# Cross-attention of layer 0 in a decoder kernel: another order of the first group's pieces, and the next stage's rows normalised apart from their turning

## The chip, the cores and the metric

The kernel runs on one core of a Trainium2 chip. The metric is the device time of one execution in microseconds. The time before the change is the median of three runs, 3578.55 us (3572.76 to 3597.9). One more execution was recorded by the hardware profiler; every view of the profile below is of that one.

The engines are named as the profile names them: PE multiplies matrices, and PEld is its loading of weights; DVE and ACT work element by element, ACT also by function tables; POOL is a third such engine; SP issues most of the DMAs. [...]

## The reference

A decoder of four layers on 16 sequences of 128 tokens with 256 features. Each layer has self-attention, cross-attention to a context of 128 x 192 per sequence, and a feed-forward part, each on the normalised x and added to x:

```python
x = x + _L0_attn_ref(_layernorm(x, axis=-1), ...)
x = x + _L0_xattn_ref(_layernorm(x, axis=-1), ctx_768, ctx_768, ...)
x = x + _L0_ffn_ref(_layernorm(x, axis=-1), ...)
...
```

The change lies in the second and at the start of the third of these. The cross-attention of layer 0 has 16 heads of 16 features. Queries come from x, keys and values from the context, each with weights and a bias. Queries and keys are divided by their lengths, over all 256 features, before the scores are taken; the softmax of the scaled scores weighs the values, and an output projection follows. The unnormalised query projection is added to that, and the sum is normalised over its features with a gain and a shift before it goes to x. The feed-forward part of layer 0 is a mixture of 32 experts and a shared one, with a router that picks eight experts for each token.

## The kernel before, in words

Tokens lie on the 128 partitions. The 2048 tokens form four groups of four sequences (`NG` = 4, `GB` = 4), so a group has 512 tokens (`GT`). x stays in on-chip memory, one tile for each group. Two kinds of PSUM buffers are used in this stage: `b1` makes single banks, four in turn, and `b2` makes double banks, two in turn.

The function `l0_xattn` gives `staggered` a prologue for each group, the scores, the exponentials and the combination of a sequence. The prologue of a group makes these pieces, in this order:

- the group's rows of x normalised (`h`, L546, on DVE);
- for two halves of the features: keys from the context (`kT`, PE), their bias (L555, DVE), their squares (`ksq`, L556, ACT);
- `h` turned by PE (`tr`), copied to `hT` by DVE (L112) and ACT (L114) in turn;
- the squared lengths of the keys, by matmuls with a single column of ones (`ksum`), clipped on DVE (L570);
- query projections of the four sequences (`qp`), their bias on DVE (L579), the sum of their squares on ACT (L580);
- lengths: maximum on DVE (L583), square root on ACT (L584), reciprocal on DVE (L585); queries divided by their lengths on ACT (`unit`, L588); output bias and shift added on POOL (L589, L590);
- values of two sequences (`v`), bias on DVE (L270);
- `unit` turned by PE (`utr`) and written as masked queries `qm`, one copy on DVE (L606), one on ACT (L607);
- values of the other two sequences.

The prologue is a generator. For group 0, `staggered` runs it to its end before anything else. For groups 1 to 3, it takes two pieces at each of the four steps of the group before. A step n takes the scores of sequence n (`st`), the last part of the combination of sequence n-3 (`proj`), the second of n-2 (`o16t`, with a reciprocal and a product `c` on DVE), a piece, the exponentials of sequence n on ACT (`e`), the first part of the combination of n-1 (`o`, copied to `oT` on ACT), another piece, and the third part of n-2 (`ctr`, copied to `cT` on DVE). After that come works that the dictionary `beside` names for this step. The last sequence of a group ends with four DVE instructions that update x (L631).

Matmuls of this stage go through `pinned` and `pinned_transpose`, which keep them in the order of the program text on PE. For the other engines a scheduler of the language orders the instructions by their dependencies and their place in the text, so an instruction can stand earlier than its line suggests.

The stage after it, `l0_ffn`, needs for each group the normalised rows of x, turned. `l0_ffn_rows(g)` does both: statistics on DVE (L653, L654), square root on ACT (L193), `nmean` on DVE (L656), rows `h` on ACT (L659), turning on PE (`tr`), copies to `hT` on ACT (L667). For groups 0 and 1 `staggered` calls it after steps 13 and 14; for groups 2 and 3 `l0_ffn` calls it after the router of groups 0 and 1. `l0_ffn` starts with the shared expert (e = -1): for each group `gate` and `up`, then `gs` on ACT (L758) and DVE (L759), then `down` of the group before, then the `router`.

The tile `h` has two buffers, which `h` of the prologue, `unit` and `h` of `l0_ffn_rows` take in turn; `hT` has five.

Of the kernel before, what the change touches and what calls it, by code (L numbers as in the profile page):

```python
# [9 lines left out]
F = mybir.dt.float32  # L10
BF = mybir.dt.bfloat16
# [6 lines left out]
P = 128  # L18
# [12 lines left out]
class Decoder:  # L31
    def __init__(self, ctx, tc, a, out):
        self.tc, self.nc, self.a, self.out = tc, tc.nc, a, out
        nc = self.nc
        pool = lambda name, bufs, **k: ctx.enter_context(tc.tile_pool(name=name, bufs=bufs, **k))
        self.const = pool("const", 1)
        self.wp = pool("weights", 1)
        self.hp = pool("hidden", 1)
        self.sm = pool("small", 4)
        self.open_psum()  # L40
        self.flip = 0
        self.l0_hT = []

        const = self.const

        self.x = []
        xv = a["x"].rearrange("(g b s) d -> g s b d", b=GB, s=P)
        for g in range(NG):
            xt = const.tile([P, GB, DM], F, tag=f"x{g}", name=f"x{g}")
            nc.sync.dma_start(out=xt, in_=xv[g])  # L50
            self.x.append(xt)
        self.col = const.tile([P, a["cols"].shape[1]], F, tag="cols", name="cols")
        nc.sync.dma_start(out=self.col, in_=a["cols"])

# [456 lines left out]
    def l0_xattn(self):  # L511
# [24 lines left out]
        with self.tc.tile_pool(name="l0x", bufs=1) as wk:  # L536
            bq, bv, bo = (self.brow(wk, f"L0_xattn_{n}") for n in ("bq", "bv", "bo"))

            def prologue(g):
# [9 lines left out]

                kT = wk.tile([P, 2, GT], F, tag="kT", name="kT", bufs=2)  # L550
                sq = self.hp.tile([P, 2, GT], F, tag="hT", name="ksq", bufs=5)
                for half in range(2):
                    ps = self.b1("kT")
                    products(ps, self.ctx_l(wk_, half * P, (half + 1) * P, slice(g * GT, (g + 1) * GT)))
                    nc.vector.tensor_scalar(kT[:, half, :], ps, self.c("L0_xattn_bk")[:, half : half + 1], None, ALU.add)  # L555
                    nc.scalar.activation(sq[:, half, :], kT[:, half, :], AF.Square)  # L556
                    yield
                hT = self.hp.tile([P, 2, GT], F, tag="hT", name="hT", bufs=5)
                for k in range(2):
                    ps = self.b1("tr")  # L560
                    for t in range(GB):
                        self.pinned_transpose(ps[:, T4(t)], h[:, t, k * P : (k + 1) * P])
                    self.evac(hT[:, k, :], ps)

                n = self.small([P, 2, GB], "lengths")
                ps = self.b1("ksum")[:, 0:GB]
                for t in range(GB):
                    products(ps[:, t : t + 1], [(sq[:, half, T4(t)], self.ones[:, 0:1]) for half in range(2)])

                nc.vector.tensor_scalar(n[:, 0], ps, 1e-24, 16.0, ALU.max, ALU.mult)  # L570
                yield
                if g % 2 == 0:
                    qps.append(self.slot([P, 2, GB, DM], "qp"))
                qp = qps[-1][:, g % 2]
                junk = wk.tile([P, DM], BF, tag="junk", name="junk", bufs=1)
                for t in range(GB):
                    ps = self.b1("qp")[:, 0:DM]
                    products(ps, [(hT[:, k, T4(t)], wq[:, k, :]) for k in range(2)])
                    nc.vector.tensor_tensor(qp[:, t, :], ps, bq, ALU.add)  # L579
                    nc.scalar.activation(junk, qp[:, t, :], AF.Square, accum_out=n[:, 1, t : t + 1])  # L580
                    if t == 1:
                        yield
                nc.vector.tensor_scalar(n[:, 1], n[:, 1], 1e-24, None, ALU.max)  # L583
                nc.scalar.activation(n, n, AF.Sqrt)  # L584
                nc.vector.reciprocal(n, n)  # L585
                u = self.hp.tile([P, GB, DM], F, tag="h", name="unit", bufs=2)
                for t in range(GB):
                    nc.scalar.activation(u[:, t, :], qp[:, t, :], AF.Copy, scale=n[:, 1, t : t + 1])  # L588
                nc.gpsimd.tensor_tensor(qp, qp, bo.unsqueeze(1).to_broadcast([P, GB, DM]), ALU.add)  # L589
                nc.gpsimd.tensor_tensor(self.x[g], self.x[g], beta.unsqueeze(1).to_broadcast([P, GB, DM]), ALU.add)  # L590
                yield
                v = []

                def values(t):
                    pairs = self.ctx_r(wv, 0, DM, slice(g * GT + t * P, g * GT + (t + 1) * P))
                    v.append(self.values32(wk, pairs, bv, products))

                values(0)
                values(1)
                yield  # L600
                qm = wk.tile([P, 2, 2, GT], F, tag="qm", name="qm", bufs=2)
                for half in range(2):
                    ps = self.b1("utr")
                    for t in range(GB):
                        self.pinned_transpose(ps[:, T4(t)], u[:, t, half * P : (half + 1) * P])
                    nc.vector.tensor_scalar(qm[:, half, 0, :], ps, self.par[:, 0:1], None, ALU.mult)  # L606
                    nc.scalar.activation(qm[:, half, 1, :], ps, AF.Copy, scale=self.par[:, 1:2])  # L607
                yield
                values(2)
                values(3)  # L610
# [2 lines left out]
            def combine(s, g, t, es):  # L613
# [25 lines left out]
                lambda s, t: self.scores16(s[0], s[1], T4(t), False),  # L639
                lambda s, t, st, nm: self.exponentials16(wk, st, s[2][:, t : t + 1], None),  # L640
                combine,
                {13: [lambda: self.l0_ffn_rows(0)], 14: [lambda: self.l0_ffn_rows(1)]},
            )

    def l0_ffn_rows(self, g):
# [12 lines left out]
        for t in range(GB):  # L658
            nc.scalar.activation(  # L659
                h[:, t, :], self.x[g][:, t, :], AF.Identity, scale=rs[:, t : t + 1], bias=nm[:, t : t + 1]  # L660
            )
        hT = self.hp.tile([P, 2, GT], F, tag="hT", name="hT", bufs=5)
        for k in range(2):
            ps = self.b1("tr")
            for t in range(GB):
                self.pinned_transpose(ps[:, t * P : (t + 1) * P], h[:, t, k * P : (k + 1) * P])
            nc.scalar.copy(hT[:, k, :], ps)  # L667
        self.l0_hT.append(hT)

    def l0_ffn(self):  # L670
# [20 lines left out]
        with self.tc.tile_pool(name="l0f", bufs=1) as wk:  # L691
# [82 lines left out]


            last, bias = None, None
            for e in range(-1, E):
                for g in range(NG):
                    now = first(e, g)
                    if last:  # L780
                        second(*last)
                    last = now
                    if e < 0:
                        router(g)
                        if g + 2 < NG:
                            self.l0_ffn_rows(g + 2)
                    if bias:
                        next(bias)
                        bias = None
                    if e == 1:  # L790
                        bias = biases(g)
                        next(bias)
# [1795 lines left out]
```

## Time and profile before

| what | value |
|---|---|
| time, median of three runs | 3578.55 us (3572.76 to 3597.9) |
| profiled execution: its time, its span | 3590.36 us, 3588.6 us |
| PE busy, share of the span | 3314.7 us, 92% |
| DVE, ACT, POOL busy | 59%, 40%, 12% |
| mean clock of PE in the span | 0.960 |
| first scores of this cross-attention start | 203.35 us |
| first `gate` of the feed-forward part starts | 340.03 us |

The span is from the first to the last instruction that the profiler saw; the execution's own time is 1.8 us longer. Times inside the span are counted from its start. In a timeline, a row is a run of like instructions on one engine: start, time from the start of the first to the end of the last, instruction, and in brackets how long the engine had been idle and which instruction ended that. A clock of 0.50 means that PE was granted half of its full clock in that stretch. Matmuls overlap, so rows of PE can begin before the row above has ended.

### The profile page before, as it was taken

The page shows a single profiled execution, that of the slowest core. Times are in us where ns is not written, and L with a number is a line of the kernel's source. Part 1 is how long each engine was busy: PE and PEld are TensorE (multiplying, and loading weights), DVE is VectorE, ACT ScalarE, POOL GpSimd, SP SyncE. Part 2 cuts the span into 40 slices and gives each one's busy share as a digit, 9 for nine tenths or more (in the row PEclk, how much of TensorE's full clock was granted, in tenths as well). Part 3 has the DMA queues.
Part 4 walks back from the last instruction along what each step waited for, and adds up shares of the span by engine and source line. Part 5 has one row for each costly group of instructions (what it writes and reads, how often), then busy time and mean ns, then how long its engine had stood idle before and what let it go on. Part 6 is the DMA issues. An engine that isn't in the chain of part 4 may idle for free.

```text
span 3588.6 us, 51453 instructions
## 1 busy us (share of the span) xinstructions
PE 3314.7 (92%) x20947; PEld 1791.9 (50%) x20947; DVE 2108.9 (59%) x4185; ACT 1428.4 (40%) x1925; POOL 424.4 (12%) x605
## 2 busy tenths in 40 slices
PE   7898999999998899998999998388999999999999
PEld 4665655555566566665555565252222222225656
DVE  5545444444554544468777544326999989964430
ACT  2356211111124422238555322024677767783221
POOL 5410000000003311110000110104000000002100
PEclk9989999999999999999999999597999999999989
DMA  2000000000010100010100000464202020000000
GB/s 78 1 23 14 14 22 18 18 23 18 28 49 2 38 1 1 1 42 8 46 1 13 3 1 1 169 209 130 35 16 32 12 31 11 11 1 26 1 8 18
DMA packets 90500, 105.46 MB, mean 29 GB/s; under 512 B 11380, under 2 KB 72694, under 8 KB 90006
## 3 DMA queue, kind: packets, MB, share of 16 engines
q1 hardware_dynamic: 79672, 89.71, 9.7%
q0 software_dynamic: 4224, 6.43, 0.6%
q10 hardware_dynamic: 6368, 6.03, 0.5%
q8 instruction: 165, 2.70, 0.3%
q14 instruction: 71, 0.58, 0.1%
HBM read 85.53 MB, written 16.60 MB: 28 GB/s over the span
## 4 chain that ended last, share of the span: by engine, by line
PE 79%; DVE 10%; ACT 5%; issue 3%; DMA 2%; POOL 1%; SPq 0%; POOLq 0%; ACTq 0%; DVEq 0%
PE acc L2120 7%; PE down L257 6%; PE gate L257 6%; PE up L257 6%; PE proj L257 6%; PE st L2120 5%; PE one L2120 4%; PE qT L168 4%; PE st L257 4%; PE o L257 2%; PE h L257 2%; DVE mx L2266 2%; PE rb L257 2%; PE v L1030 2%; PE fc L168 2%
## 5 line engine op out<-in xcount | busy, mean ns | idle before, releaser
L2266 DVE TENSOR_REDUCE mx<-one 128x1 f32<-128x512 f32 x1024 | 658.4, 686 | 58.9 <-PE one L2120 50.0
L2403 ACT ACTIVATE e<-st 128x1024 f32<-128x1024 f32 x512 | 497.1, 1021 | 209.4 <-PE st L2120 207.9
L758 ACT ACTIVATE gs<-gate,cols 128x512 f32<-128x512 f32 x132 | 90.7, 687 | 552.6 <-PE gate L257 552.5
L2120 PE MATMUL acc<-e,v 128*32 128x512 f32 x2048 | 285.6, 612 | 0.9 <-ACT e L2403 0.9
L2120 PE MATMUL st<-qp,kp 113*128 113x512 bf16 x1024 | 272.3, 386 | 5.9 <-DMA qp<-shifts 3.6
L772 DVE SCALAR_TENSOR_TENSOR x<-down,w_all,x 128x256 f32<-128x256 f32 x512 | 212.4, 478 | 110.6 <-PE down L257 110.4
L257 PE MATMUL down<-expert,gs 128*128 128x256 f32 x1056 | 250.1, 380 | 2.2 <-DVE gs L759 2.2
L257 PE MATMUL gate<-hT,expert 128*128 128x512 f32 x528 | 250.0, 596 | 0.0
L257 PE MATMUL up<-hT,expert 128*128 128x512 f32 x528 | 248.1, 592 | 0.0
L257 PEld LDWEIGHTS down<-expert,gs 128*128 128x128 f32 x1056 | 200.9, 190 | 85.8 <-issue 61.2
L759 DVE SCALAR_TENSOR_TENSOR gs<-up,cols,gs 128x512 f32<-128x512 f32 x132 | 99.0, 750 | 233.2 <-PE up L257 229.2
L2120 PE MATMUL one<-kp,qp 16*128 16x512 bf16 x1024 | 211.3, 396 | 3.7 <-DVE mx L2266 2.4
L2120 PEld LDWEIGHTS <-qp 16*128 16x128 bf16 x1024 | 48.8, 91 | 327.4 <-issue 322.6
L257 PEld LDWEIGHTS up<-hT,expert 128*128 128x128 f32 x528 | 100.3, 190 | 126.3 <-issue 126.3
L2120 PEld LDWEIGHTS <-kp 113*128 113x128 bf16 x1024 | 79.0, 98 | 143.9 <-issue 82.2
L1130 ACT COPY rb<-rb 128x512 f32<-128x512 f32 x64 | 37.5, 585 | 257.1 <-PE rb L257 257.1
L257 PEld LDWEIGHTS gate<-hT,expert 128*128 128x128 f32 x528 | 100.6, 192 | 70.8 <-issue 64.3
L1132 DVE TENSOR_TENSOR cT<-o,rb 128x512 f32<-128x512 f32 x64 | 44.3, 692 | 154.7 <-ACT rb L1130 154.7
L168 PE MATMUL qT<-hT,L_xattn_Wq 128*128 128x512 f32 x256 | 114.1, 598 | 6.9 <-DVE hT L112 4.5
L257 PE MATMUL o<-e,v 128*32 128x128 f32 (+1 forms) x2048 | 105.5, 279 | 12.6 <-DVE nm L294 11.8
L1439 DVE SCALAR_TENSOR_TENSOR xs<-xBC,cols,xs 128x508 f32<-128x508 f32 x144 | 106.0, 742 | 12.3 <-ACT xs L1435 9.0
L257 PEld LDWEIGHTS o<-e,v 128*32 128x32 f32 (+1 forms) x2048 | 81.5, 124 | 28.5 <-POOL e L335 12.3
(536 smaller groups left out, 5413.2 us busy)
## 6 DMA issues: line engine op xcount, KB each, us to landing
W<-in_L_ffn_W_dram SPq DMA_DIRECT2D x46, 512.0 KB, 5.2
expert<-in_L_ffn_Wg_dram SPq DMA_DIRECT2D x32, 128.0 KB, 2.1
expert<-in_L_ffn_Wu_dram SPq DMA_DIRECT2D x32, 128.0 KB, 2.5
expert<-in_L_ffn_Wd_dram SPq DMA_DIRECT2D x32, 128.0 KB, 2.5
parts<-parts SPq DMA_DIRECT2D x16, 256.0 KB, 2.5
qp<-parts SPq DMA_DIRECT2D x28, 128.0 KB, 3.8
kp<-parts SPq DMA_DIRECT2D x12, 256.0 KB, 8.6
hs<-zero SPq DMA_DIRECT2D x23, 128.0 KB, 1.9
```

What stands on the lines that cost most here:

```text
L168: self.nc.tensor.matmul(out, lhsT, rhs, start=i == 0, stop=i == n - 1 and bias is None)
L257: self.tc.keep_in_program_order(self.nc.tensor.matmul(*a, **k))
L758: nc.scalar.activation(gs, pg, AF.Silu, bias=bg)
L759: nc.vector.scalar_tensor_tensor(gs, pu, bu, gs, ALU.add, ALU.mult)
L772: nc.vector.scalar_tensor_tensor(xt, pd[:, t, :], w_all[:, o : o + 1], xt, ALU.mult, ALU.add)
L1030: nc.tensor.matmul(ps, l, r, start=True, stop=False)
L1130: nc.scalar.copy(rb, ps)
L1132: nc.vector.tensor_tensor(cT, po, rb, ALU.mult)
L1439: stt = lambda *a: pin(nc.vector.scalar_tensor_tensor(*a))
L2120: self.tc.keep_in_program_order(nc.tensor.matmul(*a, **k))
L2266: nc.vector.tensor_reduce(mx[:, t, kc, i : i + 1], pair[i], AX.X, ALU.max)
L2403: nc.scalar.activation(e[:, 2 * p : 2 * p + 2, :], ps, AF.Exp, scale=1.0 / 16.0)
```

## The change

The prologue's pieces become functions of their own: `keys(half)`, `turned()`, `key_lengths()`, `queries(t)`, `units()`, `values(t)`, `masked(u)`. For groups 1 to 3 they are called in the order of before, with the same places at which the generator yields. For group 0 they are called in another order: rows turned and queries first, then keys and their lengths, units, all four values, and masked queries last.

`l0_ffn_rows` is cut in two. It ends with the rows `h`, which it keeps in a dictionary; the new `l0_ffn_turn` turns and copies them. Groups 0 and 1 have their rows made after steps 10 and 12 and turned after steps 13 and 15; the rows of group 2 are made after step 16, those of group 3 at the start of the expert loop; these two are turned where both were done before. Tiles are the same as before, in shape and in number of buffers.

```diff
-        self.l0_hT = []
+        self.l0_h, self.l0_hT = {}, []
...
+                def keys(half):
                     ps = self.b1("kT")
                     products(ps, self.ctx_l(wk_, half * P, (half + 1) * P, slice(g * GT, (g + 1) * GT)))
                     nc.vector.tensor_scalar(kT[:, half, :], ps, self.c("L0_xattn_bk")[:, half : half + 1], None, ALU.add)
                     nc.scalar.activation(sq[:, half, :], kT[:, half, :], AF.Square)
-                    yield
...
+                def masked(u):
+                    for half in range(2):
+                        ps = self.b1("utr")
+                        for t in range(GB):
+                            self.pinned_transpose(ps[:, T4(t)], u[:, t, half * P : (half + 1) * P])
+                        nc.vector.tensor_scalar(qm[:, half, 0, :], ps, self.par[:, 0:1], None, ALU.mult)
+                        nc.scalar.activation(qm[:, half, 1, :], ps, AF.Copy, scale=self.par[:, 1:2])
+
+                if g == 0:
+                    turned()
+                    for t in range(GB):
+                        queries(t)
+                    keys(0)
+                    keys(1)
+                    key_lengths()
+                    u = units()
+                    for t in range(GB):
+                        values(t)
+                    masked(u)
+                    return qm, kT, n[:, 0], v, qp
+                keys(0)
+                yield
+                keys(1)
+                yield
+                turned()
+                key_lengths()
+                yield
+                queries(0)
+                queries(1)
+                yield
+                queries(2)
+                queries(3)
+                u = units()
+                yield
                 values(0)
                 values(1)
                 yield
...
+                masked(u)
                 yield
                 values(2)
                 values(3)
...
-                {13: [lambda: self.l0_ffn_rows(0)], 14: [lambda: self.l0_ffn_rows(1)]},
+                {
+                    10: [lambda: self.l0_ffn_rows(0)],
+                    12: [lambda: self.l0_ffn_rows(1)],
+                    13: [lambda: self.l0_ffn_turn(0)],
+                    15: [lambda: self.l0_ffn_turn(1)],
+                    16: [lambda: self.l0_ffn_rows(2)],
+                },
...
+        self.l0_h[g] = h
+
+    def l0_ffn_turn(self, g):
+        h = self.l0_h[g]
         hT = self.hp.tile([P, 2, GT], F, tag="hT", name="hT", bufs=5)
         for k in range(2):
             ps = self.b1("tr")
             for t in range(GB):
                 self.pinned_transpose(ps[:, t * P : (t + 1) * P], h[:, t, k * P : (k + 1) * P])
-            nc.scalar.copy(hT[:, k, :], ps)
+            self.nc.scalar.copy(hT[:, k, :], ps)
         self.l0_hT.append(hT)
...
             last, bias = None, None
+            self.l0_ffn_rows(3)
             for e in range(-1, E):
                 for g in range(NG):
...
-                            self.l0_ffn_rows(g + 2)
+                            self.l0_ffn_turn(g + 2)
```

More of the change, by code (lines that the diff above doesn't have):

```diff
@@ L551, in prologue @@
                 sq = self.hp.tile([P, 2, GT], F, tag="hT", name="ksq", bufs=5)
-                for half in range(2):
+                hT = self.hp.tile([P, 2, GT], F, tag="hT", name="hT", bufs=5)
+                if g % 2 == 0:
+                    qps.append(self.slot([P, 2, GB, DM], "qp"))
+                qp = qps[-1][:, g % 2]
+                n = self.small([P, 2, GB], "lengths")
+                qm = wk.tile([P, 2, 2, GT], F, tag="qm", name="qm", bufs=2)
+                v = []
+                def keys(half):
                     ps = self.b1("kT")
@@ L556, in prologue, with turned, key_lengths, queries @@
                     nc.scalar.activation(sq[:, half, :], kT[:, half, :], AF.Square)
-                    yield
-                hT = self.hp.tile([P, 2, GT], F, tag="hT", name="hT", bufs=5)
-                for k in range(2):
-                    ps = self.b1("tr")
-                    for t in range(GB):
[L562 to L576, printed above, removed]
+                def turned():
+                    for k in range(2):
+                        ps = self.b1("tr")
+                        for t in range(GB):
+                            self.pinned_transpose(ps[:, T4(t)], h[:, t, k * P : (k + 1) * P])
+                        self.evac(hT[:, k, :], ps)
+                def key_lengths():
+                    ps = self.b1("ksum")[:, 0:GB]
+                    for t in range(GB):
+                        products(ps[:, t : t + 1], [(sq[:, half, T4(t)], self.ones[:, 0:1]) for half in range(2)])
+                    nc.vector.tensor_scalar(n[:, 0], ps, 1e-24, 16.0, ALU.max, ALU.mult)
+                def queries(t):
                     ps = self.b1("qp")[:, 0:DM]
@@ L579, in prologue, with units @@
                     nc.vector.tensor_tensor(qp[:, t, :], ps, bq, ALU.add)
+                    junk = wk.tile([P, DM], BF, tag="junk", name="junk", bufs=1)
                     nc.scalar.activation(junk, qp[:, t, :], AF.Square, accum_out=n[:, 1, t : t + 1])
[L581 to L592, printed above, removed]
+                def units():
+                    nc.vector.tensor_scalar(n[:, 1], n[:, 1], 1e-24, None, ALU.max)
+                    nc.scalar.activation(n, n, AF.Sqrt)
+                    nc.vector.reciprocal(n, n)
+                    u = self.hp.tile([P, GB, DM], F, tag="h", name="unit", bufs=2)
+                    for t in range(GB):
+                        nc.scalar.activation(u[:, t, :], qp[:, t, :], AF.Copy, scale=n[:, 1, t : t + 1])
+                    nc.gpsimd.tensor_tensor(qp, qp, bo.unsqueeze(1).to_broadcast([P, GB, DM]), ALU.add)
+                    nc.gpsimd.tensor_tensor(
+                        self.x[g], self.x[g], beta.unsqueeze(1).to_broadcast([P, GB, DM]), ALU.add
+                    )
+                    return u
                 def values(t):
@@ L596, in values @@
                     v.append(self.values32(wk, pairs, bv, products))
+                def masked(u):
[7 more added lines that the diff above has]
+                    turned()
+                    for t in range(GB):
+                        queries(t)
[3 more added lines that the diff above has]
+                    u = units()
+                    for t in range(GB):
+                        values(t)
[15 more added lines that the diff above has]
+                yield
                 values(0)
@@ L600, in prologue @@
                 yield
[L601 to L607, printed above, removed]
+                masked(u)
                 yield
```

## The prediction

> **What bounds the kernel now.** I read the page first, for the whole span, then stretches of 5 us for the stage that the diff touches (about 180 to 360 us), then the timelines of PE, DVE and ACT there. Two rows of the page: PE's busy tenths and its clock, in 40 slices of 89.7 us.
>
> ```profile
> PE   7898999999998899998999998388999999999999
> PEclk9989999999999999999999999597999999999989
> ```
>
> PE is nearly always busy, so what PE waits for, or does at a lower clock, is time. The changed stage is the end of the second slice to the fourth. Its stretches (after the span and its length: busy us of PE, weight loads, DVE, ACT, POOL; then PE's clock, the DMA share, GB/s):
>
> ```profile
> 200.00:205.00 5.00, 5.00 (x22) 2.61 (x22) 0.85 (x2) 1.91 (x2) 2.31 (x2) 0.50 0.02 3
> ...
> 220.00:225.00 5.00, 5.00 (x41) 4.05 (x42) 0.59 (x2) 0.65 (x2) 0.44 (x2) 0.50 0.00 0
> ...
> 320.00:325.00 5.00, 0.98 (x3) 0.42 (x3) 2.38 (x8) 3.36 (x8) 0.00 (x0) 0.98 0.00 0
> ...
> 345.00:350.00 5.00, 1.80 (x7) 0.92 (x7) 4.57 (x29) 4.53 (x9) 0.00 (x0) 0.87 0.24 69
> ```
>
> From 198.8 to 226.1 PE is full but at half clock; at 320 and 345 it is empty. PE's timeline says why (start, duration, instruction; in brackets the idle time before it and who ended it):
>
> ```profile
> 184.91 1.09 PE L260 MATMUL tr<-ident,h 128*128 128x128 f32 x8
> ...
> 186.48 1.72 PE L257 MATMUL ksum<-ones,ksq 128*128 128x1 f32 x14 [0.36 <-ACT ksq L556]
> 188.06 5.39 PE L257 MATMUL qp<-L_xattn_Wq,hT 128*128 128x256 f32 x16
> 193.29 2.48 PE L257 MATMUL v<-L_xattn_Wq,ctx 128*128 128x256 f32 x8
> 196.93 2.18 PE L260 MATMUL utr<-ident,unit 128*128 128x128 f32 x8 [1.17 <-ACT unit L588]
> 198.91 4.51 PE L257 MATMUL v<-L_xattn_Wq,ctx 128*128 128x256 f32 x8
> 203.35 2.09 PE L257 MATMUL st<-qm,kT 32*128 32x256 f32 x16
> ...
> 323.63 0.33 PE L260 MATMUL tr<-ident,h 128*128 128x128 f32 x1 [3.82 <-ACT h L659]
> ...
> 348.33 0.33 PE L260 MATMUL tr<-ident,h 128*128 128x128 f32 x1 [3.00 <-ACT h L659]
> ...
> 359.30 1.88 PE L257 MATMUL gate<-hT,expert 128*128 128x512 f32 x4
> ```
>
> The first score matmuls (st) start at 203.35 behind pieces that wait for ACT (unit), and the next stage's turning (tr) waits twice for its normalised rows (ACT h). From 360 us to the next stage PE runs without a gap, so what is won here should stay won.
>
> [...] summed over 1-us stretches, half clock lasts 3.4 us at 188, 27.3 us (8 windows) at 198.8, 3.4 at 325 and 3.4 at 349, each after a wait named above. [...] 198.8 to 222 is 100% busy and yet does not recover. Those windows hold v and kT, half of whose matmuls load only 64 rows, and the one-column ksum; recovery came with the full-row qp at 222 to 226. [...]
>
> **The change, part by part.** Instruction counts on PE, DMAs and their order on SP stay; no matmul is added. For groups 1 to 3 the pieces keep their order. Against the order before, only these places move.
>
> *First group.* New order on PE: tr, qp, kT, ksum, all of v, utr, st. I lay it out from 180.8, where kT started, at full clock.
> - tr 1.09, to 181.9. It was covered by the kT matmuls; now qp waits for both copies hT. Before, from the start of tr (184.91) to the end of the second copy took 2.0 (186.33+0.57−184.91). So qp at 182.8: a wait of 0.9 us is added.
> - qp x16: twice the 1.89 that x8 takes at full clock (292.29) = 3.8, to 186.6. Its DVE adds need bq, issued at 181.10 and 3.0 us on its way: 184.1, about when the first result is there. PSUM's four small buffers cover that; nothing taken.
> - kT x8 4.1, to 190.7. ksum needs kT added on DVE (0.75) and squared on ACT (0.63): before, from kT's end at 184.97 to ksum at 186.48 took 1.5, two thirds of it covered by tr. Now tr is gone: 1.5 idle, then ksum 1.8, to 193.9.
> - v x16, twice 2.5, to 198.9. Beneath it lengths, square root and unit: the reciprocal stands behind two v adds on DVE (second at 196.8), unit takes 1.71, ready at 198.7. The 1.17 wait of utr goes.
> - utr 1.05, to 199.95. qm was covered by half of v; now st waits for it: from utr's end (199.1) to qm's end (ACT 199.28+1.34=200.6) was 1.5; half of st can start before: 1.1. st at 201.1, its end 202.2, against 205.4.
> So the new order removes 1.17+0.36 of waits and adds 0.9+1.5+1.1: by itself about 2 us worse. All else is clock. Idle plus ksum give a weak stretch of 3.25 us (190.7 to 193.9)[...]; before, the weakest was about 2.3 (195.8 to 198.1). The traced falls came after windows whose real work I put at about 35% (before 188.35: tr 0.9 and qp 0.3 of 3.41). [...] I expect the clock to fall here too, some 4 us earlier, with v (64-row half) and kT behind it, which did not recover it. Then v x16 takes 2 x 4.51 = 9.0, utr 2.0, qm's wait 0.7, st 2.1: about 193.9+13.8 = 207.7 to 208.3 against 205.4: +2.6. From there to qp of group 1 as before. If it doesn't fall: −3.2 at this point, and kT to the third st costs 10.8 at full clock (kT 4.26, st 1.08, tr 0.9, ksum 1.77, o 1.0, qp 1.83, rows of group 3) instead of 20.6: −9.8. Bounds of this part: −13 to +4 (ksum cold too). I take +2.6.
>
> *Rows of the next stage.* Rows 0 and 1 are normalised some 3 and 2 steps earlier, turned apart at 13 and 15. Their DVE statistics (four times about 0.55) move from 303–308, where they held ctr back 0.91 (309.91), to gaps near 273 and 303. On ACT, h (2.07) now stands before exponentials of step 10: 2.07 later, with 5.5 us of slack to its reader; I allow the scores at 310, whose buffers wait for step 12's exponentials, 0.6, and 0.2 near 273. Sum +0.8−0.9: take 0 to +0.7.
> At 319.8, where tr waited, the order now is st, proj, o16t, o, ctr, tr, proj. Waits left: c after the four x updates on DVE (0.5), then the chain of 2.6 from proj to ctr twice, as before, plus 0.3 for two small DVE instructions put before c. Steps: st 319.8, proj 320.8, o16t 321.8, o 322.3, ctr 323.9, tr 324.25, proj 325.2, ctr 327.8, proj 328.75, ctr 331.65, proj 332.6, gate 333.55, against 340.03: −6.5. Of that 3.82+0.5 are the wait, some 1.7 the cold window after it.
> In the ffn, rows 2 stand ready at 332.9, so tr at 348.33 (3.00 wait, then another 1.7 of cold) waits for nothing. Rows 3 stand after the fourth group's x: statistics to 339, h on ACT behind two table loads at about 345.6, tr due at 346.6: free. What is late next is gs of group 1 on ACT, behind the tables, and its buffers: 0.5 twice. gate of group 2 at 348.6, 15.05 after the first gate; before 359.30−340.03 = 19.27: −4.2.
> Boundary: −6.5−4.2+0.7 = −10.0.
>
> **Sum.** The profiled execution took 3590.36 (span 3588.6). +2.6−10.0 = −7.4 gives 3583.0. The median of the runs shown is 3578.55, 11.8 lower (their spread is 25): the same −7.4 from it gives **3571**.
>
> **Rivals.**
> 1. *The first group stays at full clock.* [...] Against: the new stretch round ksum. −13−10 = −23: **3555**.
> 2. *That, and later half-clock stretches with busy PE fall better* (the page's clock dips in the slices near 2415 to 2510, and 3435 to 3460). They are no part of the change[...]. Half of 24 to 48 us: another −15 to −20: **3538**.
> 3. *Slower: the cold stretch of the first group lasts longer.* Place: ksum at 192, after kT with nothing between. It starts colder and earlier, and misses the dense qp at about 225, so it goes on past step 3. Each window at half clock costs 1.7. Decides from (10.0−2.6)/1.7, four to five windows more; with eight more (27 us): +6 net: **3585**.
> 4. *The turning is no gain:* the two stalls come back as waits for c and for ACT's table loads, −2 in place of −10, with +2.6: **3579**. Against it: rows 1 lie ready since about 313, and no other reader needs them.
>
> **Chances.** Forecast 0.50, rival 1 0.19, rival 2 0.18, rival 3 0.08, rival 4 0.05. Within 1% is 3543 to 3614, about what a measurement of this kernel can tell from no change. Rival 2 and the low tail of rival 1 (0.03) lie below: faster 0.21; of rival 3 half above with scatter of the runs: slower 0.04; the rest same. The range reaches from between rivals 1 and 2 to above rival 3: 3544 to 3590.
>
> **What would show it.** Right: tr of rows 1 after ctr without ACT h before it; gate about 6 us, gate of group 2 about 10 us earlier relative to the step before 319; an idle 1.5 before ksum, and half clock from about 193. Wrong: full clock from 193 to 215 (rival 1); st of step 13 or c waiting over 1 us for ACT; tr of rows 3 waiting for h.

## The result and the profile after

The changed kernel takes 3571.74 us (median of 22 runs, 3560.22 to 3583.61), the kernel before 3580.19 us on the same chip (median of 22, 3571.93 to 3597.9). The ratio is 0.9972 with a 95% interval of 0.9961 to 0.9983: 6 to 14 us less. The forecast was 3571, −7.4 us.

The profiled execution shows more: 3571.38 against 3590.36, −19.0 us. So the first question is which of these 19 us belong to the change.

The two rows of the page (PE's busy tenths, and its clock), 40 slices of 89.2 us:

```profile
PE   7999999999998899998999997388999999999999
PEclk9999999999999999999999999697999999999989
```

PE's second and fourth slices and the clock's third have gone from 8 to 9. The stretches of 5 us, in the same columns as before, say where the low clock is left:

```profile
200.00:205.00 5.00, 5.00 (x14) 2.87 (x14) 3.56 (x6) 1.41 (x4) 2.34 (x1) 0.50 0.00 0
...
210.00:215.00 5.00, 5.00 (x27) 2.05 (x27) 1.50 (x2) 1.88 (x4) 0.00 (x0) 0.98 0.00 0
...
315.00:320.00 5.00, 4.62 (x66) 3.51 (x62) 4.52 (x16) 4.96 (x8) 0.00 (x0) 1.00 0.00 0
...
340.00:345.00 5.00, 5.00 (x31) 3.65 (x30) 3.72 (x18) 4.92 (x8) 0.00 (x0) 1.00 0.00 0
```

The two empty places of before, at 320 and 345, are nearly full and at full clock. One stretch at half clock is left in this stage, from 193.1 to 210.2: 17.1 us, where before had four stretches of 37.5 us together. PE's timeline of the changed kernel has the steps that the prediction laid out:

```profile
181.59 1.04 PE L260 MATMUL tr<-ident,h 128*128 128x128 f32 x8
182.98 3.72 PE L257 MATMUL qp<-L_xattn_Wq,hT 128*128 128x256 f32 x16 [0.35 <-DVE hT L112]
186.54 4.18 PE L257 MATMUL kT<-ctx,L_xattn_Wq 128*128 128x512 f32 x8
190.65 0.38 PE L257 MATMUL ksum<-ones,ksq 128*128 128x1 f32 x2
192.23 2.36 PE L257 MATMUL ksum<-ones,ksq 128*128 128x1 f32 x14 [1.19 <-ACT ksq L565]
194.45 9.25 PE L257 MATMUL v<-L_xattn_Wq,ctx 128*128 128x256 f32 x16
203.63 1.97 PE L260 MATMUL utr<-ident,unit 128*128 128x128 f32 x8
206.39 2.09 PE L257 MATMUL st<-qm,kT 32*128 32x256 f32 x16 [0.80 <-ACT qm L611]
...
299.22 1.32 PE L257 MATMUL v<-L_xattn_Wq,ctx 128*128 128x256 f32 x4 [1.20 <-ACT qm L611]
...
319.03 1.04 PE L260 MATMUL tr<-ident,h 128*128 128x128 f32 x8
...
328.20 1.88 PE L257 MATMUL gate<-hT,expert 128*128 128x512 f32 x4
...
334.65 1.98 PE L257 MATMUL gate<-hT,expert 128*128 128x512 f32 x4 [0.24 <-ACT hT L712]
...
342.66 1.88 PE L257 MATMUL gate<-hT,expert 128*128 128x512 f32 x4
```

At 319.03 the turning of rows 1 stands behind `ctr` and waits for nothing. In the first group the waits are new ones: 0.35 before `qp`, 1.19 inside `ksum`, 0.80 before the first `st`.

To place the 19 us I count from the start of the last `proj` of the self-attention, which no part of the change touches (179.82 before, 180.63 after). In the table "third st" is the first place after the whole disturbed stretch of the first group, "gate 0" the first `gate` of the feed-forward part, "gate 2" that of group 2. All come from PE's timeline.

| from the last proj, us | before | after | difference | forecast |
|---|---|---|---|---|
| first st | 23.53 | 25.76 | +2.2 | +2.6 |
| third st | 46.17 | 39.58 | −6.6 | +2.6 |
| third st to gate 0 | 114.04 | 107.99 | −6.1 | −5.8 |
| gate 0 to gate 2 | 19.27 | 14.46 | −4.8 | −4.2 |
| gate 2 | 179.48 | 162.03 | −17.5 | −7.4 |

Up to the first `st`, and from the third on, the trace does what was forecast. Between them lies a surprise of −9.2 us (from +2.6 to −6.6): half clock lasted 17.1 us in the first group, not 27.3. (The rest of the 19 us: +0.8 before the stage, −2.3 after it.)

In both traces the clock changes only on a grid of 3.413 us. Every stretch at half clock but the last of each trace, which reaches past the end of the span, is 1 to 24 times 3.413 us long (21 stretches before, 17 after), and all their beginnings and ends lie within 0.1 us of the grid. A window, below, is one step of the grid of that trace; 17.1 and 27.3 us are five and eight of them.

### The profile page after: what moved, and what is told of

The parts are those of the page before. It is cut to its first block, busy times and chain, and to the rows that moved or that the text cites. A ratio compares the mean times of both kernels' runs of the same rounds, so it can differ in the third digit from the quotient of the medians.

```text
span 3569.7 us, 51436 instructions
## 1 busy us (share of the span) xinstructions
PE 3297.9 (92%) x20930; PEld 1787.4 (50%) x20947; DVE 2106.1 (59%) x4185; ACT 1426.3 (40%) x1924; POOL 424.5 (12%) x605
## 4 chain that ended last, share of the span: by engine, by line
PE 79%; DVE 10%; ACT 5%; issue 3%; DMA 2%; POOL 1%; SPq 0%; POOLq 0%; ACTq 0%; DVEq 0%
PE acc L2166 7%; PE down L257 6%; PE gate L257 6%; PE up L257 6%; PE proj L257 6%; PE st L2166 5%; PE one L2166 4%; PE qT L168 4%; PE st L257 4%; PE o L257 2%; PE h L257 2%; DVE mx L2312 2%; PE rb L257 2%; PE fc L168 2%; PE pr L168 2%
## 5 line engine op out<-in xcount | busy, mean ns | idle before, releaser
L257 PE MATMUL gate<-hT,expert 128*128 128x512 f32 x528 | 248.6, 593 | 0.2 <-ACT hT L712 0.2
```

What stands on the lines that cost most here:

```text
L257: self.tc.keep_in_program_order(self.nc.tensor.matmul(*a, **k))
```

## The experiments

My theory after this: the rows hold the gain of about 10 us (each pair removes one stall of PE, with 3.4 us at half clock behind it); the new order is worth nothing by itself, since it still lets PE fall to half clock at `ksum`; and how long PE stays there depends on where the windows lie in that execution. Rivals: the order gives the gain, by a shorter stretch at half clock; one pair of rows alone gives it; the place of the turning, not the early rows, gives it.

All kernels in one table; times from the last `proj` as above. Half clock is that up to the third `st`.

| kernel | ratio to before, 95% interval | half clock, us | first st | third st | third st to gate 0 | gate 0 to gate 2 |
|---|---|---|---|---|---|---|
| before | 1 | 3.4 + 27.3 | 23.53 | 46.17 | 114.04 | 19.27 |
| before, again | one run | 3.4 + 17.1 | 23.25 | 41.30 | 114.85 | 19.75 |
| after | 0.9972 (0.9961 to 0.9983) | 17.1 | 25.76 | 39.58 | 107.99 | 14.46 |
| after, again | one run | 17.1 | 25.91 | 39.58 | 107.99 | 14.46 |
| rows only | 0.9962 (0.9946 to 0.9978) | 3.4 + 6.8 | 23.03 | 36.46 | 108.00 | 14.45 |
| order only | 1.0004 (0.9989 to 1.0019) | 34.1 | 25.20 | 47.62 | 113.93 | 20.91 |
| late rows undone | 1.0000 (0.9982 to 1.0017) | 27.3 | 26.16 | 44.39 | 108.54 | 19.58 |
| early rows undone | 0.9997 (0.9981 to 1.0012) | 17.1 | 26.02 | 39.58 | 114.15 | 14.46 |
| rows 1 turned in step 14 | 0.9990 (0.9976 to 1.0004) | 27.3 | 26.13 | 44.40 | 108.81 | 14.45 |
| ksum covered | 0.9949 (0.9927 to 0.9971) | 3.4 | 19.29 | 33.03 | 108.03 | 14.45 |
| full rows | 0.9947 (0.9928 to 0.9966) | 6.8 | 23.66 | 35.31 | 104.97 | 14.45 |
| ksum covered, full rows | 0.9942 (0.9922 to 0.9962) | 0 | 17.53 | 29.17 | 104.98 | 14.45 |
| before, full rows | 0.9965 (0.9952 to 0.9977) | 3.4 | 20.08 | 31.50 | 110.91 | 19.80 |

### The rows alone, and the order alone

The changed kernel without its branch for the first group:

```diff
-                if g == 0:
-                    turned()
-                    ...
-                    return qm, kT, n[:, 0], v, qp
                 keys(0)
```

> Rows and turning as in the changed kernel, the first group's pieces in the old order. My theory: the rows hold nearly the whole gain, so 10 us under the kernel before (ratio 0.997); first gate about 6 us and gate of group 2 about 10.8 us earlier after the third st than before; in the first group half clock from about 198 after the wait of utr. Rival (the order holds the gain): within 3 us of before. Rival (both needed): between.

It takes 3569.5 us, ratio 0.9962: 8 to 19 us under the kernel before, where 10 were expected. The rows alone give all that the whole change gives. The distance from the third `st` to gate 2 is 122.45 us, to the hundredth that of the changed kernel. PE's timeline of this kernel at the first group is that of the old order, with its two waits:

```profile
187.10 1.72 PE L257 MATMUL ksum<-ones,ksq 128*128 128x1 f32 x14 [0.36 <-ACT ksq L565]
...
197.55 1.96 PE L260 MATMUL utr<-ident,unit 128*128 128x128 f32 x8 [1.17 <-ACT unit L594]
...
203.47 2.09 PE L257 MATMUL st<-qm,kT 32*128 32x256 f32 x16
```

and yet its second half-clock stretch lasted 6.8 us where before had 27.3, with the same instructions in the same order.

The other way round, the new order with the rows in their old place:

```diff
                 {
-                    10: [lambda: self.l0_ffn_rows(0)],
-                    12: [lambda: self.l0_ffn_rows(1)],
-                    13: [lambda: self.l0_ffn_turn(0)],
-                    15: [lambda: self.l0_ffn_turn(1)],
-                    16: [lambda: self.l0_ffn_rows(2)],
+                    13: [lambda: self.l0_ffn_rows(0), lambda: self.l0_ffn_turn(0)],
+                    14: [lambda: self.l0_ffn_rows(1), lambda: self.l0_ffn_turn(1)],
                 },
 ...
-            self.l0_ffn_rows(3)
 ...
+                            self.l0_ffn_rows(g + 2)
                             self.l0_ffn_turn(g + 2)
```

> The first group's new order alone; rows and turning as before. My theory: waits exchanged for waits, clock falls at ksum: between 3 us slower and 3 us faster than before; PE idle about 0.35 before qp, 1.2 before ksum, 0.8 before st; both stalls for h (3.8 and 3.0 us) still there. Rival (the order wins its time by a shorter cold stretch): 6 us faster or more.

3584.06 us, ratio 1.0004: between −4 and +7 us. The forecast's +2.6 lies inside, the rival's −6 does not. Both stalls of the boundary are there in its timeline:

```profile
325.36 0.33 PE L260 MATMUL tr<-ident,h 128*128 128x128 f32 x1 [3.83 <-ACT h L697]
...
349.93 0.33 PE L260 MATMUL tr<-ident,h 128*128 128x128 f32 x1 [3.00 <-ACT h L697]
```

In this execution the new order had 34.1 us at half clock, twice the 17.1 of the changed kernel's trace. So the −6.6 at the third `st` is no property of the order.

### Each pair of rows undone

Rows 2 and 3 back in their old place, rows 0 and 1 as changed:

```diff
-                    16: [lambda: self.l0_ffn_rows(2)],
 ...
-            self.l0_ffn_rows(3)
 ...
+                            self.l0_ffn_rows(g + 2)
                             self.l0_ffn_turn(g + 2)
```

> The changed kernel with the rows of groups 2 and 3 made where they were before, after the router of groups 0 and 1. My theory: the stall of tr for h comes back (3.0 us and about 1.7 of half clock), 19.3 instead of 14.5 us from the first gate to that of group 2; the 6 us up to the first gate stay; 4 to 5 us over the changed kernel. Rival (the gain at the first gate is lost again as well, because tables on ACT come in another order): 10 us over the changed kernel.

The stall is back where it was expected, and gate 0 to gate 2 takes 19.58 us again. Its timeline:

```profile
341.39 0.33 PE L260 MATMUL tr<-ident,h 128*128 128x128 f32 x1 [3.00 <-ACT h L699]
```

From the third `st` to gate 2 it takes 128.12 us, 5.7 more than the changed kernel: 5.1 between the gates, and 0.55 before gate 0, where this trace has one window (3.4 us) at half clock at 304.85. The gain at gate 0 stays, so the rival falls. The whole, at a ratio of 1.0000 against 0.9972, would be 10 us more (3 to 17 by the two intervals), above the 4 to 5 that I expected. So I undid the other pair as well:

```diff
-                    10: [lambda: self.l0_ffn_rows(0)],
-                    12: [lambda: self.l0_ffn_rows(1)],
-                    13: [lambda: self.l0_ffn_turn(0)],
-                    15: [lambda: self.l0_ffn_turn(1)],
+                    13: [lambda: self.l0_ffn_rows(0), lambda: self.l0_ffn_turn(0)],
+                    14: [lambda: self.l0_ffn_rows(1), lambda: self.l0_ffn_turn(1)],
```

> The changed kernel, with rows 0 and 1 of the next stage normalised and turned at once in steps 13 and 14, as before; rows 2 and 3 stay where the change put them. My theory (each pair of rows removes one stall, by being ready before it is due): the wait of tr for h, 3.8 us, and about 1.7 us of half clock after it come back between the third st and the first gate, so that this distance is about 113 to 114 us, as in the kernel before, where the change has 107.99; the distance from the first gate to that of group 2 stays at 14.5. The whole is 5 to 6 us over the changed kernel, about 3577. Rival (the gain is in the late rows, to which the one-sided undoing of those rows gave nearly the whole difference): no stall, or one that another wait was hiding, and a time within 2 us of the changed kernel.

The timeline, one stall of 3.83 us and nothing in front of group 2:

```profile
317.33 2.81 PE L260 MATMUL tr<-ident,h 128*128 128x128 f32 x8 [3.83 <-ACT h L698]
...
333.83 1.88 PE L257 MATMUL gate<-hT,expert 128*128 128x512 f32 x4
...
348.29 1.88 PE L257 MATMUL gate<-hT,expert 128*128 128x512 f32 x4
```

Third `st` to gate 0 is 114.15 us (113 to 114 expected), gate 0 to gate 2 14.46 (14.5 expected). The rival, that the late rows hold the gain, falls. The stage adds up to within 1 us: early rows undone +6.2 us, late rows undone +5.7 (5.1 without the window at 304.85), both undone (the kernel before) +10.9. The profiled executions agree too: 3577.64 against 3571.38, +6.3, with the same 17.1 us at half clock in both.

The medians of whole runs don't add up so well: each undoing alone seems to cost the whole gain, +9 us here (2 to 16 by the two intervals). 5 to 6 us are inside both intervals, so this doesn't contradict the stage; but a sum of two such differences would be about 19 us, and the measured sum is 10. Why the medians overshoot is open. The half clock after 420 us, in stages that the change doesn't touch, is one thing that moves them: 234.9 and 225.2 us in the two traces of the changed kernel, 248.6 with the late rows undone, 242.0 with the early ones, 214.9 to 248.6 over all traces. The 34 us between the least and the most cost up to 17 us, by an estimate from the clock of 0.50 (`v` x16 took 9.25 us at half clock in the changed kernel and 4.99 at full clock with `ksum` covered). In the traces, what comes after gate 2 took 9.6 us longer with the late rows undone than in the changed kernel (3236.6 and 3227.0 us to the end of the span), and 0.6 longer with the early ones undone. One trace of each kernel doesn't tell what is typical for it.

### The turning in another place

```diff
-                    15: [lambda: self.l0_ffn_turn(1)],
+                    14: [lambda: self.l0_ffn_turn(1)],
```

> The changed kernel, with the turning of rows 1 in step 14, where it was before, and not in step 15; the rows themselves stay in steps 10 and 12. If it is the early normalising that removes the stall, the turning finds h ready here too: no wait of tr, third st to first gate 107 to 109 us, time within 2 us of the changed kernel. Rival (the place of the turning removes the stall): the wait of tr of 3.8 us is back, and the time is 5 us longer.

No wait of `tr`, 108.81 us to gate 0: it is the early normalising. (One window at half clock at 305.5 can explain the 0.8 us more than in the changed kernel; it came after the 1.21 us wait of `v` that the changed kernel has too.) The time does not settle it as well. By its ratio, 0.9990 against 0.9972, it is 6 us above the changed kernel (0 to 13 by the two intervals), more than the 2 that I expected and near the 5 of the rival; but the wait that the rival needs is not in the trace. The profiled execution is 6.6 us longer, 4.8 of that before the third `st`, where half clock lasted 27.3 us and not 17.1.

### The changed kernel and the kernel before once more

> The changed kernel once more, unchanged, one look. If the length of the half-clock stretch of the first group is set by where the clock's windows happen to fall, and not by the order, it may be anything from 7 to 34 us here, beginning again at about 193; if the order sets it, it is again 17.1 us, to one window. The distance from the third st to the gate of group 2 is again 122 to 123 us in either case.

> The kernel before once more, for its clock. If the length of half clock in the first group is set by where the windows fall, it differs from the 27.3 us of the first record while the order of instructions is the same; if it is set by the order, it is 27.3 again.

The changed kernel: 17.1 us again, from 192.7, as expected if the order sets it. That alone would speak for the order. The kernel before, however, had 17.1 us now, after 27.3 in the first trace, from the same program. With where the half clock began, counted from the last `proj`, the traces fall in line:

| order of the first group | half clock begins | lasts |
|---|---|---|
| new: late rows undone; rows 1 in step 14 | 12.05; 12.11 | 27.3; 27.3 |
| new: early rows undone; after again; after | 12.22; 12.34; 12.49 | 17.1; 17.1; 17.1 |
| new: order only | 13.11 | 34.1 |
| old (second stretch): before; before again; rows only | 18.72; 19.02; 19.23 | 27.3; 17.1; 6.8 |

The same order of the first group, windows shifted by up to 0.5 us, and the stretch is 6.8 to 27.3 us long in the old order; in the new one, with up to 1.1 us of shift, 17.1 to 34.1. In these traces its length went with where the windows lie, and neither order alone fixed it. (The rows are traces of single executions; how often each length comes can't be had from them.)

By the table, the windows of the changed kernel and those with the late rows undone lie 0.44 us apart. The window with the first `st`, in the one and then in the other (PE's busy time is the first figure after the length):

```profile
206.77:210.19 3.42, 3.42 (x18) 1.24 (x14) 0.00 (x0) 3.29 (x4) 0.62 (x1) 0.50 0.03 5
```

```profile
205.87:209.28 3.41, 2.96 (x17) 1.63 (x18) 0.44 (x1) 3.20 (x4) 1.45 (x1) 0.50 0.02 5
```

In the first, PE is busy throughout (3.42 us), since the wait for `qm` ended before it; full clock came at its end. In the second, 0.45 us of that wait lie inside, and half clock went on for three windows more. That these 0.45 us kept the clock low is not shown by two traces. The wait of `v` is a second case. In the changed kernel it lies across a boundary, at 298.93; with rows 1 turned in step 14 it lies in one window:

```profile
295.52:298.93 3.41, 2.50 (x39) 1.41 (x36) 3.24 (x10) 3.40 (x4) 0.09 (x1) 1.00 0.01 2
298.93:302.35 3.42, 3.13 (x24) 1.93 (x25) 1.72 (x7) 2.83 (x5) 0.00 (x0) 1.00 0.00 0
```

```profile
302.05:305.46 3.41, 2.20 (x9) 0.98 (x8) 1.88 (x6) 3.39 (x6) 0.00 (x0) 1.00 0.00 0
```

Split into 0.92 and 0.29 us, the wait was followed by full clock; 1.21 us in one window were followed by half clock.

### What would take the half clock away

If the fall comes from idle plus `ksum`, then `ksum` behind dense work should not fall. In the branch for the first group:

```diff
                     turned()
-                    for t in range(GB):
-                        queries(t)
                     keys(0)
                     keys(1)
+                    queries(0)
+                    queries(1)
                     key_lengths()
+                    queries(2)
+                    queries(3)
                     u = units()
```

> The changed kernel with group 0 in the order rows turned, keys, two queries, key lengths, two queries, units, values, masked: the wait of ksum is covered by queries, ksum (1.8 us) stands between full-row matmuls. My theory (idle plus ksum pull the clock down there): no wait before qp and ksum, so 1.5 us less at full clock; no lasting half clock near 193, so the first st some 6 to 7 us earlier after its first tr than in the changed kernel (25 us there), and 5 to 10 us under the changed kernel in all. Rival (the clock falls by chance, whatever the order): half clock there as before, 1 to 2 us under the changed kernel.

PE's timeline:

```profile
186.54 1.99 PE L257 MATMUL qp<-L_xattn_Wq,hT 128*128 128x256 f32 x8
188.37 1.84 PE L257 MATMUL ksum<-ones,ksq 128*128 128x1 f32 x16
190.08 1.97 PE L257 MATMUL qp<-L_xattn_Wq,hT 128*128 128x256 f32 x8
191.89 4.99 PE L257 MATMUL v<-L_xattn_Wq,ctx 128*128 128x256 f32 x16
...
199.88 1.89 PE L257 MATMUL st<-qm,kT 32*128 32x256 f32 x16 [1.13 <-ACT qm L611]
```

The waits of 0.35 and 1.19 are gone, `v` takes 4.99 us instead of 9.25, and the first `st` starts 6.5 us earlier. Only the wait for `qm` still costs one window, 3.4 us at 200.4. So the fall at 193 went with `ksum` standing bare behind a wait (1.19 us in the changed kernel).

The edit takes away the wait and covers `ksum` at once. Two windows of the kernel before tell them apart in part: the first holds `tr`, 16 `ksum` and 0.36 us of idle time, and was followed by half clock; the second holds `o16t`, `o` and `ctr` with 1.63 us of idle time, and was not.

```profile
184.88:188.29 3.41, 3.05 (x26) 2.94 (x26) 1.40 (x3) 1.10 (x2) 0.00 (x0) 1.00 1.03 285
318.00:321.41 3.41, 1.78 (x38) 1.13 (x36) 2.88 (x10) 3.32 (x6) 0.00 (x0) 1.00 0.00 0
```

So in this trace the idle time of a window alone did not decide. The ratio is 0.9949; against the changed kernel that is 8 us with an uncertainty of the same size.

The prediction put the failure to recover on matmuls with 64 rows of weights. To test that, the second matmul of each pair of `kT` and `v` is given 128 rows, the lower 64 of them zero:

```diff
-    def ctx_l(self, w, lo, hi, cols):
+    def ctx_l(self, w, lo, hi, cols, k=DC - P):
 ...
-        return [(w[:, 0, lo:hi], self.ctx0[:, cols]), (w[0 : DC - P, 1, lo:hi], self.ctx1[0 : DC - P, cols])]
+        return [(w[:, 0, lo:hi], self.ctx0[:, cols]), (w[0:k, 1, lo:hi], self.ctx1[0:k, cols])]
 ...
+        for w in (wk_, wv):
+            nc.gpsimd.memset(w[DC - P : P, 1, :], 0.0)
 ...
-                    products(ps, self.ctx_l(wk_, ..., slice(g * GT, (g + 1) * GT)))
+                    products(ps, self.ctx_l(wk_, ..., slice(g * GT, (g + 1) * GT), P))
```

and the same for `ctx_r` and `v`. Nothing else is computed than before: what is added is products with zero.

> The changed kernel with the second matmul of kT and v in this cross-attention over 128 rows in place of 64: the lower 64 rows of that weight chunk are zero, the context already lies there twice. Same number and shape of results, same time of a matmul. My theory (weak rows hold the clock down): the clock still falls at ksum, but recovers after one window of 3.4 us within v, not after five; st some 5 us earlier, 5 to 8 us under the changed kernel in all. Rival (rows don't matter to the clock): cold for 17 to 27 us as before, within 2 us of the changed kernel.

Half clock lasts 6.8 us, two windows (one was expected), in place of five. Two windows were also seen without full rows, in the kernel with the rows only, so this one trace does not show that weak rows hold the clock down. The other expectation, matmuls that take the same time, was wrong: they are faster. From its timeline:

```profile
186.21 3.60 PE L257 MATMUL kT<-ctx,L_xattn_Wq 128*128 128x512 f32 x8
...
203.97 1.37 PE L257 MATMUL st<-qm,kT 32*128 32x256 f32 x16 [3.14 <-ACT qm L614]
...
291.84 1.13 PE L257 MATMUL v<-L_xattn_Wq,ctx 128*128 128x256 f32 x4 [2.11 <-ACT qm L614]
```

`kT` takes 3.60 us where the changed kernel, also at full clock, takes 4.18. Part of that comes back as waits for `qm`: 3.14 us before the first `st` (0.80 in the changed kernel), 2.11 at `v` (1.20). So the gain, by the ratios' middle 19 us on the kernel before and 9 on the changed one, can't be put down to the clock alone. The same edit on the kernel before:

> The kernel before with matmuls over 128 rows for kT and v in this cross-attention, nothing else changed. My theory: half clock after utr ends after one or two windows in place of eight: 5 to 9 us under the kernel before (ratio 0.998). Rival (rows help only the changed order): within 2 us of before.

The kernel before, then the same with full rows, both at full clock:

```profile
295.13 2.58 PE L257 MATMUL v<-L_xattn_Wq,ctx 128*128 128x256 f32 x8
```

```profile
192.95 1.89 PE L257 MATMUL v<-L_xattn_Wq,ctx 128*128 128x256 f32 x8
196.53 1.96 PE L260 MATMUL utr<-ident,unit 128*128 128x128 f32 x8 [1.69 <-ACT unit L591]
198.33 1.89 PE L257 MATMUL v<-L_xattn_Wq,ctx 128*128 128x256 f32 x8
```

2.58 us (2.48 in the first group) become 1.89, and after the 1.69 us wait before `utr`, longer than the 1.17 that preceded the fall in the kernel before, the clock did not fall at all there. But here the wait lies across a boundary of the windows, at 195.69, half on each side, and the 1.17 us lay within one window. So it is not shown whether the full rows kept the clock up or the place of the windows did. The whole ratio is 0.9965, 8 to 17 us under the kernel before, where 5 to 9 were expected; the faster matmuls were not in that sum.

Both edits together, on the changed kernel:

> The covered order of the first group and matmuls over 128 rows together, with the changed kernel's rows. My theory: both act on the same half-clock stretch, so they don't add: within 3 us of each alone, some 7 to 10 us under the changed kernel and 15 to 19 under the one before. Rival (they act on different stretches): another 7 us under either.

3558.62 us, ratio 0.9942, 14 to 28 us under the kernel before. By the ratios' middles it is 2 us under each edit alone, within the 3 expected: the two hardly add. It has the lowest ratio of all. From the last `proj` to gate 2 it takes 148.60 us (before 179.48, after 162.03) without any half clock. Its intervals and those of each edit alone overlap.

## Why the prediction was right

**First group, up to the first score matmuls: as laid out.** The fall of the clock at `ksum`, forecast for "about 193", came at 193.1, and in all seven traces of the new order (full rows among them) between 192.2 and 193.2. That idle time and `ksum` together would bring it down was my estimate from the falls in the trace of before. Measured against forecast: wait of `qp` 0.35 and 0.9; of `ksum` 1.19 and 1.5; of `st` for `qm` 0.80 and 1.1; `v` at half clock 9.25 and 9.0; the first `st` later by 2.2 and 2.6. The waits were each a little smaller, since PE did the first two matmuls of `ksum` while the second half of the squares was made, and the copies `hT` were done sooner.

**First group, after that: this step failed for the traced execution.** "From there to qp of group 1 as before" took the 8 windows (27.3 us) of one trace for a fixed length. It was 5 in the changed kernel, 8, 5 and 2 with the old order, 5, 8 and 10 with the new one. The term was mis-sized by −9.2 us in this trace and by nothing that can be told in the medians: the order alone measured +1.4 us (−4 to +7), forecast +2.6. That is most of why the profile shows −19.0 and the medians −8.4. What keeps the clock low stays open. The prediction named the 64-row and one-column matmuls, and a recovery with the full-row `qp`; in the changed kernel full clock came at 210.2, after a window of `st` and two `kT`, before any `qp` of group 1, and the full rows do not decide it.

**Rows of the next stage: right, but for where a small wait fell.** Third `st` to gate 2 went down by 10.9 us, forecast 10.0. The stall of 3.82 and its window at half clock went (−6.1 with what the earlier rows cost, forecast −5.8), the stall of 3.00 with its own went (−4.8, forecast −4.2). Undoing each pair brought back just its part. The allowance of 0 to +0.7 for earlier rows came about right in size and at other places: not the scores at 310 waited, but `v` at 299.22, for 1.20 us, and `st` for 0.30, less the 0.91 of `ctr` that went. Net +0.6. ACT's timeline of the changed kernel says how (a change of function table, ACT_TABLE_LOAD, takes 1.28 us in it):

```profile
293.08 2.08 ACT L700 ACTIVATE h<-x,nmean,rstd 128x256 f32<-128x256 f32 x4
295.18 1.28 ACT L330 ACT_TABLE_LOAD   x1
296.47 2.12 ACT L330 ACTIVATE e<-st,lengths 128x1024 f32<-128x1024 f32 x2
298.48 1.27 ACT L611 ACTIVATE qm<-utr,par 128x512 f32<-128x512 f32 x2
```

`h` of rows 0 now stands ahead of the exponentials, and `qm` behind them; `v` waits 1.20 us for the PSUM buffer that `qm` still reads. With rows 0 back in step 13, `v` waits for nothing, and the 0.91 of `ctr` is there again.

**What was late next.** `ctr` waited 0.38 for the c of step 13 (0.5 forecast). Of the two waits of 0.5 for `gs` none came, only 0.24 for a copy `hT`. The tiles `h` of rows 3, due with 1 us to spare by the forecast, ended on ACT at 340.28, before their `tr` at 341.62.

**The rivals.** The first group at full clock (1 and 2) did not come: every trace of the new order fell. That it can be had is shown by the covered `ksum`, which needs another order than the one made. Rival 3, eight windows more, didn't come; the longest stretch, 34.1 us in the order alone, is ten windows, two more than in the first trace of the kernel before. Rival 4 fell with each pair of rows.

**The number.** That the measured 3571.74 lies within 1 us of the forecast 3571 is luck. The gain is known to 6 to 14 us, and the kernel before measured 1.6 us above the median that the forecast started from. For the profiled execution 3583.0 was forecast and 3571.38 measured.

## What to carry to other kernels

A wait of PE for normalised rows cost more than its length here: with the 3.4 us at half clock behind it, 3.8 us of wait were worth about 6 and 3.0 about 5, and it went when the part on other engines was put steps earlier while the turning stayed where PE has room. Before a stretch at half clock is booked as won or lost, see in a second trace of the same program how long it is; here it was 17.1 or 27.3 us. Where the one-column matmuls were laid between dense ones, in two traces, the clock did not fall there. Filling a half-empty second matmul up with zero rows made the pairs faster here; that it also keeps the clock up is not shown.

## What the runs showed of the hardware

- PE stayed at half clock for two to ten windows in the first group (6.8 to 34.1 us): for 27.3 us in the kernel before without any idle time, and for 17.1 us in the changed one with one wait of 0.8 us. In these stretches are pairs of matmuls with 128 and 64 rows of weights, one-column matmuls and `st`. What ends them is not shown.
- The window before the fall at 188.3 in the kernel before had 0.36 us of idle time of 3.41, that before the fall at 193.1 in the changed one 1.19. More idle time was not always followed by a fall: with full rows, 1.95 us idle between 199.37 and 202.78 were followed by full clock.
- The boundaries of the windows keep a period of 3.413 us through the whole execution, to 0.1 us, in the traces of the kernel before and of the changed one. Counted from the span's start and with whole periods taken off, they lay at 0.6 to 2.4 us in the 12 traces that have half clock in the first group. So where a wait fell against the windows was not the same each time; whether that is random, 12 traces don't settle.
- Filling the second matmul of a pair up from 64 to 128 rows made the pairs faster, not slower: `kT` x8 3.60 us in place of 4.18, `v` x8 1.89 in place of 2.58, and `v` x4 1.13 in place of 1.32, so 0.10 to 0.17 us for each pair. Why is not shown.
